# Row maxima of attention scores as b + relu(a - b) on two engines, and the output bias as a row added by TensorE

## Chip, cores and metric

One core of a Trainium2 chip runs the whole decoder layer. The time is the device time of one execution in microseconds. Three executions of the kernel before took 5262.17, 5269.80 and 5275.28 us, median 5269.8 us. The engines are called PE (TensorE), ACT (ScalarE), DVE (VectorE), POOL (GpSimd) and SP (SyncE, which here only issues DMAs). Each of them works its own queue in order.

## What is computed

Three sub-layers follow one another for x of shape (8, 512, 512). Each adds its result to its input and normalizes. The first is a selective state-space layer: a recurrence over 512 positions for 1024 channels with 16 states each. The second is cross-attention with 16 heads of 32. The third is a mixture of 32 experts with a shared expert. All is float32. The change is in the attention:

```python
qm = _split_heads(q @ Wq.T + bq)
km = _split_heads(k @ Wk.T + bk)
vm = _split_heads(v @ Wv.T + bv)
scores = jnp.einsum('bnlh,bnph->bnlp', qm, km) / np.sqrt(HEAD_DIM).astype(np.float32)
scores = jnp.where(mask, scores, MASK_FILL)
attn = jax.nn.softmax(scores, axis=-1)
out = jnp.einsum('bnlp,bnph->bnlh', attn, vm)
out = out.transpose(0, 2, 1, 3).reshape(B, L, D_MODEL)
return out @ Wo.T + bo
...
h = dA_t * h + dBx_t            # the recurrence of the first sub-layer, 512 positions
...
x = _layernorm(x + _L0_attn_ref(x, ...))
x = _layernorm(x + _L0_xattn_ref(x, ctx_1024, ctx_1024, mask_BxS2_bf1, ...))
x = _layernorm(x + _L0_ffn_ref(x, ...))
```

## The kernel before

Three functions run in turn. `layers` does the state-space layer, the attention, the shared expert and the choice of experts, `experts` the 32 experts, and `finish` the last normalization. The change touches `layers` alone.

`layers` goes over 16 chunks of 256 positions (8 batch rows, two chunks each). A chunk has 32 scan steps, 512 in all. One scan step (L1113 to L1208) is, in program order:

- `steps_in` (L494, DVE): the input of the recurrence, 128 x 1024, into a tile `h` (tag h, 6 buffers).
- `scan` (L501, DVE): the recurrence over 128 x 1028. It reads decays `l_da`, which has two buffers.
- `decays` (L480, ACT): four exponentials of 128 x 256 that fill the other decay buffer for the next step. They can start only when the scan that last read this buffer has ended.
- `collect` (L510, DVE): 128 x 1024, times C. Then `products` (L521, PE) folds pairs of `h` tiles into PSUM `py`, after which an `h` tile is free again.

Everything else is side work, put into the steps in small pieces. The attention and the shared expert of batch row b run beside the scans of row b + 1; for the last row they run after the last scan. `units(b)` lists those pieces with a weight each, and the step loop (L1148 to L1153) takes from the list in proportion to weights. The pieces of a step are dealt into thirds (L1154), and each third is issued by `run(m)`: the first before the scan, the second after the decays, the third after `collect`. `clock[0]` counts these thirds. A piece may return a function that is its second half; `settle` (L294) issues it when the next piece runs, or, where a pair (due, function) is returned, when `clock[0]` has reached `due`. The code is issued through a scheduler that settles the order on each engine when the kernel is built; at run time every engine takes its queue in that order and waits on semaphores.

The attention of one batch row has 8 head pairs, and each pair 4 blocks of 128 query rows. For pair i:

- `spread` (L799): DMAs put the pair's queries and keys into `qa` and `ka` (three sets of each). A head takes 64 rows: 32 of the head, one with the mask's fill `filld` in `ka`, one of ones in `ka` against the negated maxima in `qa`.
- `maximum` (L811): two matmuls (L819) make 128 x 2 x 512 scores `ps_s` in PSUM (tag sc, 2 buffers), and one DVE reduction (L821) takes the largest of each row and head into `mx`.
- `negate` (L823): transposes `mx` and puts it, negated, as a row into `qa`.
- `weigh` (L839): two matmuls (L845) make the scores again, transposed and with the maximum already subtracted, `ps_t` (same tag sc), and ACT takes their exponential into `eT` (L849; tag eT, 2 buffers).
- `gather` (L853): two matmuls (L861) multiply by the values.

A maximum, a weigh and a gather of different pairs stand together in the list (L997 to L1008), the maximum six blocks ahead. I call the three a group; there are 32 in a batch row and 256 in all, 224 of them beside scans.

`sources(b)` makes keys and values a row ahead and spills them to DRAM (`keys`, L732, four blocks per batch row). `output` (L908) multiplies by Wo through `dense` (L753) and adds the residual (L919) and the bias `bo` (L920), the latter a tile of 128 x 512 that holds the bias in every row. `biases` (L1037) prepares `bo` and `filld` once. `silu` (L391) is preceded and followed by a load of ACT's function table.

Of the kernel before, what the change touches and what calls it, by code (L numbers as in the profile page):

```python
# [8 lines left out]
F32 = mybir.dt.float32  # L9
# [8 lines left out]
P = 128  # L18
# [14 lines left out]
NB = 4  # L33
NPB = 3

NH = 16
# [53 lines left out]
def layers(ctx, tc, a, x1d, filld, based, xbuf, arm):  # L90
# [88 lines left out]
    w_x = const("w_x", [P, CC, RANK + 2 * NST], rows(a["x_proj_w"]))  # L179
    w_dt = const("w_dt", [RANK, DI], a["dt_proj_w"])  # L180
    b_dt = const("b_dt", [P, CC], a["dt_proj_b"])
# [4 lines left out]
    bv = cp.tile([P, DC], F32, name="l_bv")  # L186
    bo = cp.tile([P, D], F32, name="l_bo")
    wg = cp.tile([P, DC, E], F32, name="l_wg")
# [47 lines left out]
    for i in range(NPB):  # L236
        qas.append(cp.tile([P, S], F32, name=f"l_qa{i}"))
        kas.append(cp.tile([P, S], F32, name=f"l_ka{i}"))
        for t in (qas[i], kas[i]):
            for r0 in (HD, 2 * HD + HD):  # L240
                nc.gpsimd.memset(t[r0 : r0 + HD], 1.0 if t is qas[i] else 0.0)
# [21 lines left out]
    def later_constants():  # L263

        nc.sync.dma_start(
            aneg.rearrange("p c j g -> p (c j) g"),
            a["A_log"].rearrange("(b c) (s g) -> (c s) b g", c=QP, s=NQ),
        )
        for i in range(NPB):
            for r0 in (HD + 1, 2 * HD + HD + 1):  # L270
                nc.sync.dma_start(
                    kas[i][r0 : r0 + 1, :].rearrange("p (c t) -> p c t", c=DC),
                    ones[0:1, :].unsqueeze(1).to_broadcast([1, DC, P]),
                )
        nc.sync.dma_start(bq, a["bq"])
        nc.sync.dma_start(bk, a["bk"])
        nc.sync.dma_start(bv, a["bv"].rearrange("(c p) -> p c", p=P))
        nc.sync.dma_start(bo, a["bo"].partition_broadcast(P))
        nc.sync.dma_start(wg, rows(a["wg"]))
# [152 lines left out]
    def prepare(q, f):  # L432

        ps = psm.tile([P, 2, T], F32, tag="mm", name="ps_dt")
        for i in range(2):
            c = 2 * q + i
            nc.tensor.matmul(
                ps[:, i, :], w_dt[:, c * P : (c + 1) * P], f["xd"][0:RANK, :], start=True, stop=True
            )
# [267 lines left out]
    def sources(b):  # L707
# [3 lines left out]
        def begin():  # L711
            load("Wv")
            st["cT"] = cT = quad("s2", "cT")
            nc.sync.dma_start(cT, rows(a["ctx"][b]))
            st["mk"] = mk = p1.tile([P, S], U8, tag="mk", name="mk")
            nc.sync.dma_start(mk, a["mask"][b : b + 1, :].to_broadcast([P, S]))
            kept[b] = [dp.tile([S, D], F32, tag="vd", name="vd"), dp.tile([D, S], F32, tag="kd", name="kd")]

# [13 lines left out]
        def keys(oc):  # L732
            if oc == 0 and b:
                load("Wq")
            w, cT = loaded["Wk"], st["cT"]
            ps = dense(lambda dc: w[:, dc, oc * P : (oc + 1) * P], lambda dc: cT[:, dc, :])

            def put():

                k = p3.tile([P, D], F32, tag="row", name="k")  # L740
                nc.vector.scalar_tensor_tensor(k, ps, bk[:, oc : oc + 1], st["mk"], ALU.add, ALU.mult)
                nc.sync.dma_start(kept[b][1][oc * P : (oc + 1) * P, :], k)

            return put
# [7 lines left out]

    def dense(lhs, rhs):  # L753
        ps = psm.tile([P, S], F32, tag="mm", name="ps_p")
        for dc in range(DC):
            nc.tensor.matmul(ps, lhs(dc), rhs(dc), start=(dc == 0), stop=(dc == DC - 1))  # L756
        return ps

    def units(b):
# [39 lines left out]
        def spread(i):  # L799
# [3 lines left out]
            for j in range(2):  # L803
# [4 lines left out]
                nc.sync.dma_start(ka[r1 + HD : r1 + HD + 1, :], filld[b : b + 1, :])  # L808
                nc.sync.dma_start(qa[r1 + HD + 1 : r1 + HD + 2, :], ka[r1 + HD + 2 : r1 + HD + 3, :])

        def maximum(i, lt):  # L811
# [5 lines left out]
            for j in range(2):  # L817
                r = slice(j * 2 * HD, (j + 1) * 2 * HD)
                nc.tensor.matmul(ps[:, j, :], qa[r, lt * P : (lt + 1) * P], ka[r, :], start=True, stop=True)  # L819
            mx = st["mx", i]  # L820
            return lambda: nc.vector.tensor_reduce(mx[:, lt, :].unsqueeze(2), ps, AX.X, ALU.max) and None  # L821

        def negate(i):  # L823

            mx = st.pop(("mx", i))
            pm = psm.tile([P, S], F32, tag="mm", name="ps_m")
            for lt in range(SC):
# [80 lines left out]
        def output(lt):  # L908
# [6 lines left out]
            w, attT = loaded["Wo"], st["attT"]  # L915
            pp = dense(lambda dc: attT[:, dc, lt * P : (lt + 1) * P], lambda dc: w[:, dc, :])

            def add_up():
                nc.vector.tensor_tensor(xr, pp, xr, ALU.add)  # L919
                nc.vector.tensor_tensor(st["x2"][lt], xr, bo, ALU.add)  # L920
                if lt == SC - 1:
# [115 lines left out]
    def biases():  # L1037
# [6 lines left out]
        nc.vector.tensor_scalar(fl[0:B, :], fl[0:B, :], -1.0, 1e8, ALU.add, ALU.mult)  # L1044
        nc.sync.dma_start(filld, fl[0:B, :])

# [3 lines left out]
        for dc in range(DC):  # L1050
# [3 lines left out]
            )  # L1054
        nc.vector.tensor_tensor(bo, bo, psb, ALU.add)

# [544 lines left out]
def program(tc, a, out):  # L1601
    nc = tc.nc
    with tc.tile_pool(name="dram", bufs=1, space=DRAM) as dram, tc.tile_pool(name="one", bufs=1) as one:
        x1d = dram.tile([N, D], F32, name="x1d")
        filld = dram.tile([B, S], F32, name="filld")

# [42 lines left out]
```

## Time and profile before

| what | us |
|---|---|
| median of three runs (5262.17 to 5275.28) | 5269.8 |
| the profiled execution | 5265.16 |
| its span, first to last instruction | 5263.4 |
| DVE busy over the span | 4170.1 (79%) |
| PE busy | 4483.6 (85%) |
| ACT busy | 2584.7 (49%) |
| POOL busy | 587.0 (11%) |
| first to last scan (start of each) | 60.6 to 3517.8 |
| attention of the last row and its shared expert, then experts and last normalization | from about 3520 |

A group line of the profile reads: line of the code, engine, operation, output <- inputs, shape, count, then busy time and mean duration in ns, then the idle time of the engine just before these instructions and what ended it. Busy time counts overlap once; so durations of neighbours can add up to more than the time they take together. A window line gives busy time and number of instructions of PE, PE's weight loads, DVE, ACT and POOL in a stretch, then the granted PE clock, DMA share and GB/s. A line of the table of waits reads: who waited, for whom, total us, times, longest. For the timeline: start, length, engine, line and operation, with neighbours of one kind merged into "xN" and the idle time before it in brackets.

### The profile page before, as it was taken

What the parts mean: (1) busy time and instruction counts of PE and PEld (TensorE: products, weight loads), DVE (VectorE), ACT (ScalarE), POOL (GpSimd) and SP (SyncE); (2) the same over time, 40 slices, a digit from 0 to 9 for tenths busy, and PEclk for the clock granted to TensorE, in tenths of its full rate; (3) what the DMA queues carried; (4) which work ended last, traced back from release to release, by engine and by line L of the source; (5) the groups of instructions that cost most, each with busy time, mean ns of one, the idle gap of its engine ahead of it and who ended that gap; (6) DMA issues with size and microseconds to landing.
All of it is one profiled execution on the core that took longest, in us unless ns stands there. A gap on an engine that the chain in (4) does not pass through costs nothing. (4 is left out here: it accounts for less than half of the span.)

```text
span 5263.4 us, 54340 instructions
## 1 busy us (share of the span) xinstructions
PE 4483.6 (85%) x17184; PEld 2454.6 (47%) x17184; DVE 4170.1 (79%) x5333; ACT 2584.7 (49%) x5765; POOL 587.0 (11%) x426
## 2 busy tenths in 40 slices
PE   6768879888888988888898888878899999999895
PEld 3324234333423423343342343333478888877775
DVE  7999898989989998998999899883356666655555
ACT  5566565655556556565656656543222333323233
POOL 1000002001100200200020020010112111111111
PEclk8879999999998999999898999989899999999998
DMA  8885345435634634543473454433244444444344
GB/s 236 265 231 156 74 118 175 116 97 135 180 83 104 200 95 107 161 142 97 95 217 74 120 176 116 107 106 106 96 116 134 133 126 134 134 124 126 116 125 157
DMA packets 486437, 711.62 MB, mean 135 GB/s; under 512 B 121576, under 2 KB 205064, under 8 KB 483952
## 3 DMA queue, kind: packets, MB, share of 16 engines
q1 hardware_dynamic: 449984, 626.90, 41.8%
q0 software_dynamic: 33280, 67.81, 5.8%
q10 hardware_dynamic: 2736, 11.54, 0.5%
q8 instruction: 220, 3.60, 0.3%
q14 instruction: 217, 1.78, 0.1%
HBM read 391.24 MB, written 164.79 MB: 106 GB/s over the span
## 5 line engine op out<-in xcount | busy, mean ns | idle before, releaser
L480 ACT ACTIVATE l_da<-rep,l_aneg 128x256 f32<-128x256 f32 x2048 | 893.4, 499 | 948.1 <-DVE h L501 884.5
L501 DVE TENSOR_TENSOR_SCAN h<-l_da,h 128x1028 f32<-128x1028 f32 x512 | 1165.1, 2290 | 20.9 <-ACT l_da L480 18.3
L494 DVE TENSOR_TENSOR h<-rep,bc 128x1024 f32<-128x1024 f32 x512 | 613.9, 1216 | 107.7 <-PE py L521 90.7
L510 DVE TENSOR_TENSOR h<-h,bc 128x1024 f32<-128x1024 f32 x512 | 618.6, 1215 | 2.0
L521 PE MATMUL py<-h,l_fold 128*32 128x512 f32 x2048 | 370.8, 647 | 110.1 <-DVE h L510 92.3
L819 PE MATMUL ps_s<-l_ka,l_qa 64*128 64x512 f32 x1024 | 329.2, 714 | 139.8 <-DVE mx L821 139.4
L1334 PE MATMUL ps_h<-xT,w 128*128 128x224 f32 (+3 forms) x1536 | 376.4, 395 | 36.8 <-issue 29.7
L1427 POOL DMA_INDIRECT based<-y,xe x160 | 272.8, 1705 | 1157.8 <-ACT y L1406 432.4
L821 DVE TENSOR_REDUCE mx<-ps_s 128x2 f32<-128x1024 f32 x256 | 310.0, 1216 | 66.5 <-PE ps_s L819 66.2
L861 PE MATMUL po<-eT,l_va 128*64 128x512 f32 x1024 | 303.6, 674 | 47.5 <-ACT eT L849 42.9
L1334 PEld LDWEIGHTS ps_h<-xT,w 128*128 128x128 f32 x1536 | 293.3, 192 | 100.3 <-issue 41.6
L845 PE MATMUL ps_t<-l_qa,l_ka 64*128 64x512 f32 x1024 | 306.0, 669 | 23.9 <-ACT eT L849 23.3
L849 ACT ACTIVATE eT<-ps_t 128x1024 f32<-128x1024 f32 x256 | 258.7, 1015 | 128.7 <-PE ps_t L845 128.5
L694 POOL DMA_INDIRECT xbuf<-x2t,dest x128 | 217.2, 1697 | 863.2 <-DVE dest L679 762.4
L343 PE MATMUL ps_z<-xnT,wm 128*128 128x256 f32 x1024 | 237.7, 388 | 28.7 <-DVE o L561 23.7
L756 PE MATMUL ps_p<-x2T,wa 128*128 128x512 f32 x512 | 242.0, 627 | 20.5 <-ACT hT L950 13.8
L552 PE MATMUL po<-wm,zs 128*128 128x512 f32 x512 | 246.7, 636 | 13.4 <-DVE z L963 11.7
L1334 PE MATMUL ps_h<-t,s 128*128 128x224 f32 (+3 forms) x1024 | 247.4, 392 | 5.8 <-DVE hT L1355 5.8
L343 PE MATMUL ps_x<-xnT,wm 128*128 128x256 f32 x1024 | 245.6, 392 | 4.9 <-ACT xnT L332 2.8
L1355 DVE TENSOR_TENSOR hT<-ps_h,p 128x224 f32<-128x224 f32 (+3 forms) x128 | 55.3, 432 | 242.7 <-PE ps_h L1334 242.7
L343 PEld LDWEIGHTS ps_z<-xnT,wm 128*128 128x128 f32 x1024 | 194.9, 193 | 90.5 <-DVE o L561 37.0
L343 PEld LDWEIGHTS ps_x<-xnT,wm 128*128 128x128 f32 x1024 | 195.5, 195 | 81.6 <-issue 44.8
(239 smaller groups left out, 6971.3 us busy)
## 6 DMA issues: line engine op xcount, KB each, us to landing
w<-in_w SPq DMA_DIRECT2D x93, 1024.0 KB
wm<-in_in_proj_w SPq DMA_DIRECT2D x128, 512.0 KB
rep<-dt SPq DMA_DIRECT2D x256, 256.0 KB
rep<-dtx SPq DMA_DIRECT2D x256, 256.0 KB
xbuf<-zero SPq DMA_DIRECT2D x32, 1362.5 KB
xe<-xbuf SPq DMA_DIRECT2D x32, 1362.5 KB
wm<-in_out_proj_w SPq DMA_DIRECT2D x64, 512.0 KB
wa<-in_sw SPq DMA_DIRECT2D x24, 1024.0 KB
```

The costliest lines, as they stand in the source:

```text
L343: nc.tensor.matmul(ps[:, i, :], w[:, dc, i * P : (i + 1) * P], f["xnT"][:, dc, :], start=(dc == 0), stop=(dc == DC - 1),)
L480: nc.scalar.activation(da[:, n, 1:], dt[:, j, i, :], AF.Exp, scale=aneg[:, 2 * q + i, 2 * jj + j, g : g + 1])
L494: nc.vector.tensor_tensor(h[:, :, 1:], dtx.rearrange("p j i t -> p (j i) t"), f["bc", g][0], ALU.mult)
L501: nc.vector.tensor_tensor_scan(flat, da.rearrange("p n t -> p (n t)"), flat, 0.0, ALU.mult, ALU.add)
L510: nc.vector.tensor_tensor(h[:, :, 0:T], h[:, :, 1:], f["bc", g][1], ALU.mult)
L521: nc.tensor.matmul(f["py"][j * QP : (j + 1) * QP, :, :], fold, hs[j // 2][:, 2 * (j % 2) : 2 * (j % 2) + 2, 0:T], start=False, stop=g == N ...
L819: nc.tensor.matmul(ps[:, j, :], qa[r, lt * P : (lt + 1) * P], ka[r, :], start=True, stop=True)
L821: return lambda: nc.vector.tensor_reduce(mx[:, lt, :].unsqueeze(2), ps, AX.X, ALU.max) and None
L845: nc.tensor.matmul(ps[:, j, :], ka[r, kc * P : (kc + 1) * P], qa[r, :], start=True, stop=True)
L861: nc.tensor.matmul(po[j * 2 * HD : (j + 1) * 2 * HD, :], va[:, kc, i, j * HD : (j + 2) * HD], eT[:, j, :], start=(kc == 0), stop=(kc == SC ...
L1334: nc.tensor.matmul(ps, w[:, n, r * P : (r + 1) * P], x[:, n, 0:cols], start=not more and n == 0, stop=n == 1, skip_group_check=more,)
L1427: put = nc.gpsimd.indirect_dma_start(out=based, out_offset=bass.IndirectOffsetOnAxis(ap=xe.bitcast(I32)[:, j, D + E :], axis=0), in_=ys[j] ...
```

## The change

The keys of a row, 512 columns, get a third half beside them: `ka` grows to 768 columns, where the last 256 hold the first half less the second half (a - b). For that `keys` subtracts once more and spills a second DMA, and `filld` gets the same third half. `maximum` now multiplies by columns 256 to 767, so that PSUM holds b and a - b instead of a and b. ACT takes relu(a - b) of both heads into a tile `up` of tag eT (128 x 2 x 256). DVE then adds b to it and takes the row maximum, once for each head, by `tensor_tensor_reduce`. In the built program each of these stands as two DVE instructions: the operation over 128 x 256, and a second one that writes `mx` (128 x 1). `ramp` hands the DVE part back with a due time one third of a step on; `negate` issues whatever is still owed.

The output bias becomes one row of a 32-row block that lies in the spare rows of the tile `w_dt`, the other 31 being zero. `dense` adds it by a fifth matmul against 32 rows of ones, and `output` is left with one DVE addition instead of two.

```diff
-    w_dt = const("w_dt", [RANK, DI], a["dt_proj_w"])
+    w_dt = cp.tile([2 * RANK, DI], F32, name="l_w_dt")
+    nc.sync.dma_start(w_dt[0:RANK, :], a["dt_proj_w"])
+    bo = w_dt[RANK : 2 * RANK, 0:D]
+    nc.gpsimd.memset(bo, 0.0)
-    bo = cp.tile([P, D], F32, name="l_bo")
...
-        kas.append(cp.tile([P, S], F32, name=f"l_ka{i}"))
+        kas.append(cp.tile([P, S + HS], F32, name=f"l_ka{i}"))
...
                 nc.vector.scalar_tensor_tensor(k, ps, bk[:, oc : oc + 1], st["mk"], ALU.add, ALU.mult)
-                nc.sync.dma_start(kept[b][1][oc * P : (oc + 1) * P, :], k)
+                nc.sync.dma_start(kept[b][1][oc * P : (oc + 1) * P, 0:S], k)
+                less = p3.tile([P, D], F32, tag="row", name="less")[:, 0:HS]
+                nc.vector.tensor_tensor(less, k[:, 0:HS], k[:, HS:], ALU.subtract)
+                nc.sync.dma_start(kept[b][1][oc * P : (oc + 1) * P, S:], less)
...
-    def dense(lhs, rhs):
+    def dense(lhs, rhs, row=None):
         ps = psm.tile([P, S], F32, tag="mm", name="ps_p")
         for dc in range(DC):
-            nc.tensor.matmul(ps, lhs(dc), rhs(dc), start=(dc == 0), stop=(dc == DC - 1))
+            nc.tensor.matmul(ps, lhs(dc), rhs(dc), start=(dc == 0), stop=(dc == DC - 1 and row is None))
+        if row is not None:
+            nc.tensor.matmul(ps, ones[RANK : 2 * RANK, :], row, start=False, stop=True)
         return ps
...
-                nc.tensor.matmul(ps[:, j, :], qa[r, lt * P : (lt + 1) * P], ka[r, :], start=True, stop=True)
+                nc.tensor.matmul(ps[:, j, :], qa[r, lt * P : (lt + 1) * P], ka[r, HS:], start=True, stop=True)
             mx = st["mx", i]
-            return lambda: nc.vector.tensor_reduce(mx[:, lt, :].unsqueeze(2), ps, AX.X, ALU.max) and None
+
+            def ramp():
+                up = p2.tile([P, 2, S], F32, tag="eT", name="up")[:, :, 0:HS]
+                nc.scalar.activation(up, ps[:, :, HS:], AF.Relu)
+
+                def largest():
+                    for j in range(2):
+                        nc.vector.tensor_tensor_reduce(
+                            up[:, j, :], ps[:, j, 0:HS], up[:, j, :], 1.0, -3e38, ALU.add, ALU.max, mx[:, lt, j : j + 1]
+                        )
+
+                owed = st.setdefault(("owed", i), [])
+                owed.append(largest)
+                return (clock[0] + 1 if clock else 0), lambda: owed and owed.pop(0)()
+
+            return ramp
 
         def negate(i):
 
             mx = st.pop(("mx", i))
+            owed = st.pop(("owed", i))
+            while owed:
+                owed.pop(0)()
...
-            pp = dense(lambda dc: attT[:, dc, lt * P : (lt + 1) * P], lambda dc: w[:, dc, :])
+            pp = dense(lambda dc: attT[:, dc, lt * P : (lt + 1) * P], lambda dc: w[:, dc, :], bo)
 
             def add_up():
-                nc.vector.tensor_tensor(xr, pp, xr, ALU.add)
-                nc.vector.tensor_tensor(st["x2"][lt], xr, bo, ALU.add)
+                nc.vector.tensor_tensor(st["x2"][lt], pp, xr, ALU.add)
...
-        nc.sync.dma_start(filld, fl[0:B, :])
+        nc.sync.dma_start(filld[:, 0:S], fl[0:B, :])
+        less = p3.tile([P, D], F32, tag="row", name="less")[0:B, 0:HS]
+        nc.vector.tensor_tensor(less, fl[0:B, 0:HS], fl[0:B, HS:], ALU.subtract)
+        nc.sync.dma_start(filld[:, S:], less)
...
-        nc.vector.tensor_tensor(bo, bo, psb, ALU.add)
+        row = p3.tile([P, D], F32, tag="row", name="bo")[0:1, :]
+        nc.sync.dma_start(row, a["bo"].unsqueeze(0))
+        nc.vector.tensor_tensor(row, row, psb[0:1, :], ALU.add)
+        nc.sync.dma_start(bo[0:1, :], row)
```

More of the change, by code (lines that the diff above doesn't have):

```diff
@@ L34 @@
 NPB = 3
+HS = S // 2
 NH = 16
@@ L271, in later_constants @@
                 nc.sync.dma_start(
-                    kas[i][r0 : r0 + 1, :].rearrange("p (c t) -> p c t", c=DC),
+                    kas[i][r0 : r0 + 1, 0:S].rearrange("p (c t) -> p c t", c=DC),
                     ones[0:1, :].unsqueeze(1).to_broadcast([1, DC, P]),
@@ L277, in later_constants @@
         nc.sync.dma_start(bv, a["bv"].rearrange("(c p) -> p c", p=P))
-        nc.sync.dma_start(bo, a["bo"].partition_broadcast(P))
         nc.sync.dma_start(wg, rows(a["wg"]))
@@ L437, in prepare @@
             nc.tensor.matmul(
-                ps[:, i, :], w_dt[:, c * P : (c + 1) * P], f["xd"][0:RANK, :], start=True, stop=True
+                ps[:, i, :], w_dt[0:RANK, c * P : (c + 1) * P], f["xd"][0:RANK, :], start=True, stop=True
             )
@@ L716, in begin @@
             nc.sync.dma_start(mk, a["mask"][b : b + 1, :].to_broadcast([P, S]))
-            kept[b] = [dp.tile([S, D], F32, tag="vd", name="vd"), dp.tile([D, S], F32, tag="kd", name="kd")]
+            kept[b] = [dp.tile([S, D], F32, tag="vd", name="vd"), dp.tile([D, S + HS], F32, tag="kd", name="kd")]
         def values(pc):
@@ L808, in spread @@
                 nc.sync.dma_start(ka[r1 + HD : r1 + HD + 1, :], filld[b : b + 1, :])
-                nc.sync.dma_start(qa[r1 + HD + 1 : r1 + HD + 2, :], ka[r1 + HD + 2 : r1 + HD + 3, :])
+                nc.sync.dma_start(qa[r1 + HD + 1 : r1 + HD + 2, :], ka[r1 + HD + 2 : r1 + HD + 3, 0:S])
         def maximum(i, lt):
@@ L1604, in program @@
         x1d = dram.tile([N, D], F32, name="x1d")
-        filld = dram.tile([B, S], F32, name="filld")
+        filld = dram.tile([B, S + HS], F32, name="filld")
         based = dram.tile([N, D], F32, name="based")
```

## The prediction

> **What bounds the kernel now.** I read the busy time by stretches first, then the costliest groups, then the waits of DVE and ACT between 500 and 3400 us, then the timeline.
>
> ```profile
> 900.00:1400.00 500.00, 423.50 (x1530) 184.96 (x1529) 449.45 (x489) 297.51 (x667) 44.13 (x31) 0.95 0.49 133
> ...
> 3600.00:3700.00 100.00, 98.72 (x412) 29.64 (x408) 44.71 (x41) 44.20 (x53) 0.00 (x0) 1.00 0.17 43
> ```
>
> Beside scans (900 to 1400) DVE is busy 449 of 500 us, PE 424, ACT 298: DVE bounds, PE is close. In the last row's attention, without scans (3600 to 3700), PE is busy 98.7 of 100: PE bounds.
>
> ```profile
> L480 ACT ACTIVATE l_da<-rep,l_aneg 128x256 f32<-128x256 f32 x2048 | 893.4, 499 | 948.1 <-DVE h L501 884.5
> L501 DVE TENSOR_TENSOR_SCAN h<-l_da,h 128x1028 f32<-128x1028 f32 x512 | 1165.1, 2290 | 20.9 <-ACT l_da L480 18.3
> L494 DVE TENSOR_TENSOR h<-rep,bc 128x1024 f32<-128x1024 f32 x512 | 613.9, 1216 | 107.7 <-PE py L521 90.7
> ...
> L821 DVE TENSOR_REDUCE mx<-ps_s 128x2 f32<-128x1024 f32 x256 | 310.0, 1216 | 66.5 <-PE ps_s L819 66.2
> ```
>
> The reductions are 310 us of DVE. ACT has 948 us of idle time before its decays alone, but it is idle because its queue's head waits for a scan; whatever stands behind those decays waits too.
>
> ```profile
> DVE h L494 <- PE py L521: 90.5, 37, 6.8
> DVE m L74 <- ACT r L70: 31.3, 25, 3.2
> DVE dtx L457 <- ACT dtx L453: 28.0, 20, 3.1
> DVE xs L377 <- ACT xs L369: 24.2, 14, 3.4
> DVE h L501 <- ACT l_da L480: 16.9, 6, 3.4
> DVE mx L821 <- PE ps_s L819: 13.3, 15, 1.4
> DVE zs L535 <- ACT zs L394: 13.0, 6, 2.2
> ```
>
> Where DVE waits for ACT today, it loses 113 us in all (31.3 + 28.0 + 24.2 + 16.9 + 13.0). The maxima wait for PE only, and little.
>
> ```profile
> 519.71 2.07 DVE L377 SCALAR_TENSOR_TENSOR xs<-xp,l_cw,xs 128x256 f32<-128x256 f32 x5
> 521.69 1.22 DVE L494 TENSOR_TENSOR h<-rep,bc 128x1024 f32<-128x1024 f32 x1
> 522.83 2.35 DVE L821 TENSOR_REDUCE mx<-ps_s 128x2 f32<-128x1024 f32 x2
> ```
>
> Neighbours overlap: the reduction lasts 1.22 us, but two take 2.35, so it occupies DVE 1.13 us. Five operations of 256 columns take 2.07, that is 0.40 each. Additions of 1024 and 512 columns occupy 1.13 and 0.60, so 1.04 ns a column, and a plain one of 256 would be 0.33.
>
> **The change, part by part.** Time counts where DVE bounds: 7 of 8 rows, so 224 of 256 maxima and 28 of 32 `output` blocks.
>
> *The maxima on DVE.* Out: 1.13 us each. In: two operations of 256 columns and two reads of the accumulator. No such operation is in the trace. Low: 0.33 + nothing, 0.67 a maximum; no two-source row runs faster than 1.04 ns a column, so it can't be less. High: the scan's rate (2290 ns for 1028 columns, 2.2 ns each), 0.63 an operation, and 0.17 a read as DVE's smallest rows last (L63 171 ns, L65 173), 1.60. I take 0.36 (between 0.33 and 0.40) and 0.10, 0.92 a maximum: it is an addition of one PSUM and one SBUF source, as L919, whose 512 columns last 682 ns like SBUF alone. 224 x (0.92 - 1.13) = **-47 us** (-103 to +105).
>
> Two scalar_tensor_tensor rows with both float32 sources in SBUF show the plain rate:
>
> ```profile
> L457 DVE SCALAR_TENSOR_TENSOR dtx<-dtx,u 128x512 f32<-128x512 f32 x64 | 43.8, 684 | 36.6 <-ACT dtx L453 36.6
> ...
> L458 DVE TENSOR_TENSOR l<-l,dtx 128x512 f32<-128x512 f32 x64 | 43.7, 682 | 1.0
> ```
>
> The Trainium skill's Vector Engine (DVE) Microarchitecture Reference, section 7 (Points that are easy to get wrong), says that this form halves its throughput with two non-bf16 SBUF sources; here 684 stands beside 682 for the plain addition, so the row doesn't show it, and by the rule a maximum would be near 1.4 us and the sum 60 us slower instead of 47 faster. Its VectorE: DVE Perf Modes, Rules for kernel authors, advises few operations rather than many; the change puts four in place of one, which the 0.92 holds already.
>
> *The bias.* One addition of 512 columns less: 28 x 0.60 = **-17 us**. PE gets 32 more matmuls of 512 columns; 18 of L756 take 7.89 us, 0.44 each, 28 x 0.44 = 12 us. I cost it at nothing: PE is idle 15% beside scans. Without that cover it is +12.
>
> *Keys.* 32 more DVE subtractions of 256 columns: **+11 us** (32 x 0.33). Their 32 DMAs, and the 256 that carry 768 columns for 512, go on SP's queue and on DMA engines that are half idle (share 0.49): nothing, as what waits for them was issued two pairs ahead. `less` takes a second `row` buffer, so a later key block may wait for a landing; at most about 1 us each, as L741 lost 1.0 to a DMA once, +28 at worst.
>
> *ACT.* 224 relus of 512 columns. L389 copies 512 columns from PSUM in 571 ns; less the overlap (four 499 ns decays take 1.69 to 1.71, so 0.09) it is 0.5: 112 us, in a queue that is idle 40% beside scans. As work it costs nothing. In the built order 16 table loads of 1.28 us are gone (128 to 112), 20 us that ACT gains.
>
> *The new waits.* DVE now waits for ACT at each maximum, and all its queue behind it: scans, `collect`, the inputs. And since `up` and `eT` share two buffers, in the built order the exponential of a group waits for DVE's part of the maximum before it, and the next relu stands behind that exponential. The stretch of the order that I copy out here repeats for nearly every row: scan; `collect`; DVE's pair; two inputs; DVE's next pair. ACT stands between the same scan and that next pair's relu with four decays, a relu, a table load, four silus, a table load, an exponential, and the relu: 4 x 0.40 + 0.5 + 1.28 + 4 x 0.54 + 1.28 + 0.92 + 0.5 = 8.2 us. DVE has 1.13 + 0.92 + 1.13 + 1.13 = 4.3 us to do. So it waits 3.9 us. Before, the reduction there didn't wait for ACT.
>
> I counted this for every DVE instruction that waits for ACT up to the last scan, in both built orders: ACT's queue from the DVE result that gates it, up to the awaited result, less what DVE has queued in between, plus 0.15 for handing over (when positive). Before: 74 us. After: 212, of which 96 at 49 of 224 maxima, and more than before at the convolution (27 to 39), at L457's chain (10 to 31) and the small normalization operations (13 to 19). The rise is 138. The same count through PE rises by 52, from 34 to 86. The count for before is under the trace's 113, so it doesn't exaggerate singly; but waits overlap, and part of the new ones falls on the 90.5 us that DVE now waits for `py`. I take three quarters of ACT's rise and none of PE's: **+104 us**. Bounds: 0 (all in idle time) to 138 x 113/74 + 52 = 263.
>
> *The last row.*
>
> ```profile
> 3643.04 1.13 PE L819 MATMUL ps_s<-l_ka,l_qa 64*128 64x512 f32 x4
> ...
> 3644.21 1.23 DVE L821 TENSOR_REDUCE mx<-ps_s 128x2 f32<-128x1024 f32 x1 [1.23 <-PE ps_s L819]
> ...
> 3645.96 0.30 PEld L819 LDWEIGHTS ps_s<-l_ka,l_qa 64*128 64x128 f32 x4 [0.81 <-DVE mx L821]
> ```
>
> A group takes 2.92 us (3643.04 to 3645.96), and PE fills it. The circle of a score buffer is 1.17 + 1.23 = 2.4 now; it becomes 1.17 + 0.5 + 0.92 and two handovers of 0.15, 2.9: the cover is used up but not passed. 32 x 0.1 + 4 x 0.44 = **+5** (0 to 15).
>
> **Sum:** -47 - 17 + 11 + 104 + 5 = +56. The profiled execution took 5265.2; with the change 5321. The median of the runs lies 4.6 above it: **5326 us**.
>
> **Rivals.**
> - *The waits fall into idle time.* For it: DVE already idles 10% beside scans, and DVE's part is issued a third of a step late. Against: 49 places where ACT has more queued than DVE. Then -53 for DVE and about 5 for the last row: 5222; with the cheap read (-103) 5166.
> - *Gain and waits cancel*, within 0.3% (16 us, about what a measurement of this kernel can tell from no change): waits of 32 to 64 us.
> - *The reduce form runs at the scan's rate.* Place: DVE, at each maximum. For it: nothing shows the operation; against: L919. From 1.13 us a maximum on, the edit saves nothing; at 1.60 it costs +105 instead of -47: 5478.
> - *PE becomes the bound*: score buffers are held longer, PE's queue stops, `py` comes late and L494 waits. For it: PE is 85% busy and its count rises by 52. Then 5326 + 52 + 34 (the rest of ACT's rise) = 5412.
> - *No saving on DVE*, if operation and read are 0.40 and 0.17 (1.14, +2 for -47): 5326 + 49 = 5375, inside the forecast's own range.
>
> **How the numbers follow.** Forecast (slower by waits, 5287 to 5440) 0.45; waits hidden 0.31; cancel 0.11; scan's rate 0.06; PE 0.07. Faster 0.31, same 0.11, slower 0.58. The range leaves out the scan's rate, the upper end of the waits and the lower third of the hidden case: 5195 to 5430.
>
> **What would show it.** L821's place: two rows of about 0.45 us and two small ones; DVE's busy time beside scans down by some 50 us. DVE waiting for ACT at the maxima, near 100 us in all, and ACT's exponentials waiting for DVE, which they never did. The scan stage (first to last scan now 60 to 3518) longer while DVE's share of it falls. Wrong if DVE's waits for ACT stay near 113 us (then faster), or if a maximum occupies DVE for 1.13 us or more (then slower for another reason).

## The result and the profile after

The changed kernel takes 5277.8 us (median of 13 runs, 5273.0 to 5286.1); the kernel before took 5263.8 beside it (13 runs). The ratio is 1.0027, 95% interval 1.0020 to 1.0035: some 14 us slower, where the forecast said about 56. The profiled execution spans 5271.8 us, 8.4 more than the one before (5263.4).

First the same two stretches of the view by stretches, for the kernel after. The columns are length, busy time of PE, PEld, DVE, ACT and POOL with instruction counts, granted clock, DMA share and GB/s.

```profile
900.00:1400.00 500.00, 436.42 (x1558) 188.80 (x1557) 436.26 (x590) 313.53 (x702) 40.96 (x30) 0.94 0.48 135
3600.00:3700.00 100.00, 97.64 (x376) 30.57 (x374) 30.68 (x132) 53.45 (x75) 0.14 (x1) 0.99 0.29 90
```

Beside scans DVE falls from 449 to 436 of 500 us while PE and ACT rise. DVE is now as busy as PE, and neither is full. The last row is still PE's (97.6 of 100).

The costliest groups of the kernel after, and from the groups of DVE the accumulator reads, which are too small for the page:

```profile
L482 ACT ACTIVATE l_da<-rep,l_aneg 128x256 f32<-128x256 f32 x2048 | 901.5, 500 | 836.0 <-DVE h L503 711.0
L503 DVE TENSOR_TENSOR_SCAN h<-l_da,h 128x1028 f32<-128x1028 f32 x512 | 1166.5, 2288 | 6.3 <-ACT l_da L482 2.4
L496 DVE TENSOR_TENSOR h<-rep,bc 128x1024 f32<-128x1024 f32 x512 | 613.5, 1214 | 145.8 <-PE py L523 130.5
...
L835 DVE CUSTOM_DVE_ANT_0 up<-ps_s,up 128x256 f32<-128x256 f32 x512 | 195.0, 417 | 186.8 <-ACT up L831 185.4
...
L874 ACT ACTIVATE eT<-ps_t 128x1024 f32<-128x1024 f32 x256 | 259.6, 1017 | 96.5 <-DVE mx L835 78.6
```

```profile
L835 DVE DVE_READ_ACCUMULATOR2_ANT mx<- 128x1 f32 x512 | 41.9, 82 | 0.0
```

The 310 us of reductions have become 195 of additions with a running maximum and 42 of reads. DVE waits 185 us for the relu in the whole span, and the exponentials of L874 wait 79 us for DVE's maxima.

What a maximum occupies is read from starts, not from durations. DVE's timeline of the kernel after (start, duration, instruction):

```profile
1009.79 0.41 DVE L835 CUSTOM_DVE_ANT_0 up<-ps_s,up 128x256 f32<-128x256 f32 x1
1010.13 0.08 DVE L835 DVE_READ_ACCUMULATOR2_ANT mx<- 128x1 f32 x1
1010.13 0.41 DVE L835 CUSTOM_DVE_ANT_0 up<-ps_s,up 128x256 f32<-128x256 f32 x1
1010.48 0.08 DVE L835 DVE_READ_ACCUMULATOR2_ANT mx<- 128x1 f32 x1
1010.48 2.29 DVE L503 TENSOR_TENSOR_SCAN h<-l_da,h 128x1028 f32<-128x1028 f32 x1
```

The read and the next operation start at the same moment. So a maximum occupies 0.69 us (1009.79 to 1010.48), not 0.92.

Waits of DVE in the scan stage of the kernel after (61.7 to 3534.3; total, times, longest), and that stage's row by stretches:

```profile
DVE h L496 <- PE py L523: 130.5, 61, 6.5
DVE up L835 <- ACT up L831: 117.7, 49, 5.7
DVE m L75 <- ACT r L71: 41.2, 26, 4.5
DVE dtx L459 <- ACT dtx L455: 22.5, 15, 3.1
DVE zs L537 <- ACT zs L396: 13.3, 7, 2.2
...
DVE xs L379 <- ACT xs L371: 3.6, 4, 2.1
DVE h L503 <- ACT l_da L482: 2.4, 1, 2.4
```

```profile
61.70:3534.30 3472.60, 2905.76 (x10195) 1220.42 (x10194) 3087.51 (x4052) 2136.06 (x4803) 256.92 (x191) 0.92 0.51 140
```

The same stage before (60.6 to 3520.1), with two of its waits:

```profile
60.60:3520.10 3459.50, 2864.43 (x10166) 1220.63 (x10164) 3185.66 (x3382) 2040.93 (x4598) 271.24 (x191) 0.92 0.50 138
```

```profile
DVE h L494 <- PE py L521: 90.7, 38, 6.8
DVE m L74 <- ACT r L70: 31.5, 26, 3.2
```

It lasted 3459.5 us with DVE busy for 3185.7. So DVE lost 98 us of work and gained 111 us of idle time (273.8 to 385.1), and the stage grew by 13. The new wait for the relu has 118 us at 49 places; the one for `py` grew from 91 to 131, the one in the normalizations (`m`) from 32 to 41. The part from the start of the last scan on went from 1745.6 to 1739.8 us. A single profile is worth about 8 us here: another execution of the very same program (the run with two thirds of a step, below) had a scan stage of 3480.2 us for 3472.6.

### The profile page after: what moved, and what is told of

Read it like the earlier page. It is cut to its first block, busy times and chain, and to the rows that moved or that the text cites. A ratio compares the mean times of both kernels' runs of the same rounds, so it can differ in the third digit from the quotient of the medians.

```text
span 5271.8 us, 55880 instructions
## 1 busy us (share of the span) xinstructions
PE 4538.0 (86%) x17248; PEld 2454.8 (47%) x17248; DVE 4057.3 (77%) x6102; ACT 2701.0 (51%) x6005; POOL 574.1 (11%) x427
## 5 line engine op out<-in xcount | busy, mean ns | idle before, releaser
L496 DVE TENSOR_TENSOR h<-rep,bc 128x1024 f32<-128x1024 f32 x512 | 613.5, 1214 | 145.8 <-PE py L523 130.5
L523 PE MATMUL py<-h,l_fold 128*32 128x512 f32 x2048 | 392.9, 672 | 106.5 <-DVE h L512 90.3
L826 PE MATMUL ps_s<-l_ka,l_qa 64*128 64x512 f32 x1024 | 316.4, 684 | 158.1 <-DVE mx L835 153.6
L835 DVE CUSTOM_DVE_ANT_0 up<-ps_s,up 128x256 f32<-128x256 f32 x512 | 195.0, 417 | 186.8 <-ACT up L831 185.4
L874 ACT ACTIVATE eT<-ps_t 128x1024 f32<-128x1024 f32 x256 | 259.6, 1017 | 96.5 <-DVE mx L835 78.6
L826 PEld LDWEIGHTS ps_s<-l_ka,l_qa 64*128 64x128 f32 x1024 | 87.0, 192 | 322.4 <-issue 144.7
```

The lines of the kernel that those rows point to most:

```text
L496: nc.vector.tensor_tensor(h[:, :, 1:], dtx.rearrange("p j i t -> p (j i) t"), f["bc", g][0], ALU.mult)
L523: nc.tensor.matmul(f["py"][j * QP : (j + 1) * QP, :, :], fold, hs[j // 2][:, 2 * (j % 2) : 2 * (j % 2) + 2, 0:T], start=False, stop=g == N ...
L874: nc.scalar.activation(eT, ps, AF.Exp)
```

## Experiments

Differences in us are the difference of two ratios times 5264, the median before, so that runs taken at different times can be set side by side. The first guess was that the 14 us are a loss by waits, less gains of the bias and of the cheap maximum.

**The bias row alone** (the kernel before with only the change's bias part):

```diff
-            pp = dense(lambda dc: attT[:, dc, lt * P : (lt + 1) * P], lambda dc: w[:, dc, :])
+            pp = dense(lambda dc: attT[:, dc, lt * P : (lt + 1) * P], lambda dc: w[:, dc, :], bo)
...
-                nc.vector.tensor_tensor(xr, pp, xr, ALU.add)
-                nc.vector.tensor_tensor(st["x2"][lt], xr, bo, ALU.add)
+                nc.vector.tensor_tensor(st["x2"][lt], pp, xr, ALU.add)
```

> The kernel before with the bias row alone; maxima and keys as before. Theory A (DVE bounds beside scans, and what leaves its queue without a new wait is gained): 28 additions that occupy DVE 0.60 us each leave, so 17 us faster, 5240 to 5255 against about 5264. Rival B (PE's fifth matmul delays what stands behind it as much as DVE gains): within 8 us of the kernel before.

Measured: 5281.2 us, 1.0031 [1.0019, 1.0043]: 16 us slower instead of 17 faster. Its scan stage, and DVE's first waits in it:

```profile
61.10:3532.80 3471.70, 2910.04 (x10197) 1230.40 (x10196) 3171.03 (x3348) 2040.68 (x4594) 261.04 (x191) 0.91 0.50 138
```

```profile
DVE h L495 <- PE py L522: 100.8, 44, 7.0
DVE m L74 <- ACT r L70: 40.3, 26, 4.0
```

DVE has its 15 us less work (3185.7 to 3171.0), but the stage is 12 longer; PE is busy for 46 more. A loss of that size was there without a single relu.

**Buffers of its own for the relu:**

```diff
-                up = p2.tile([P, 2, S], F32, tag="eT", name="up")[:, :, 0:HS]
+                up = p2.tile([P, D], F32, tag="xr", name="up").rearrange("p (j k) -> p j k", j=2)
```

> The changed kernel with relu's result in two buffers of its own (the two of tag xr, idle during the maxima) instead of the two that it shares with the exponentials. In the built order 175 of 256 exponentials wait for DVE's part of a maximum in the changed kernel, and none here. Theory A1 (the 118 us that DVE waits for relu come mostly of this sharing, relu standing behind an exponential that stands behind DVE): the wait of DVE for relu falls under 60 us and the time to 5200 to 5240. Rival A2 (relu is late because of ACT's own queue, decays that wait for scans, and table loads): the wait stays above 90 us and the time at 5265 to 5285.

Measured: 5280.4 us, 1.0033 [1.0023, 1.0042]. DVE still waits 116.0 us for the relu, at 52 places. The shared buffers are not the cause. In the changed kernel's trace, ACT stands before a relu for want of scores in under 2 of the 118 us that DVE waits; some 29 are the relus themselves, and in the rest ACT is at instructions ahead of them or waits there. So the relu is late because of what stands before it in ACT's own queue.

**No relu.** ACT's relu is left out; DVE adds ones to b, so the maximum is over half the keys and carries no relu.

```diff
-                up = p2.tile([P, 2, S], F32, tag="eT", name="up")[:, :, 0:HS]
-                nc.scalar.activation(up, ps[:, :, HS:], AF.Relu)
+                pass
...
-                            up[:, j, :], ps[:, j, 0:HS], up[:, j, :], 1.0, -3e38, ALU.add, ALU.max, mx[:, lt, j : j + 1]
+                            junk[:, j], ps[:, j, 0:HS].rearrange("p (n k) -> p n k", n=2), two, 1.0, -3e38, ALU.add, ALU.max, mx[:, lt, j : j + 1]
```

> The changed kernel without relu: DVE adds a constant tile to b instead, so the maximum goes over half of the keys and ACT does nothing for it. Theory A (DVE's 98 us of saved work are real, and waiting for ACT takes them back): 5150 to 5190. Rival C (what DVE saves is taken back by PE, whose score buffers and in-order queue set the pace): 5230 or more, with more idle time of DVE before L496 for PE.

Measured: 5219.8 us, 0.9911 [0.9895, 0.9927]: 61 us under the changed kernel. The wait for the relu (118 us) is gone, and only about half of it comes back as time. Where the rest went is in DVE's waits of this run:

```profile
DVE h L496 <- PE py L523: 133.3, 64, 5.8
DVE m L75 <- ACT r L71: 41.6, 26, 4.6
DVE dtx L459 <- ACT dtx L455: 35.4, 17, 3.1
DVE h L503 <- ACT l_da L482: 28.0, 7, 4.8
DVE junk L836 <- PE ps_s L826: 14.0, 15, 2.1
```

Decays, `dtx` and scores (2.4, 22.5 and nothing in the changed kernel) now take 28, 35 and 14 us. This run's built order also has 14 more loads of ACT's function tables than the changed kernel's (123 and 109 in the traces, 1.28 us each), so ACT is relieved of the relus less 18 us.

**The relu made, but unread** (DVE reads ones, as above; the maximum is again over half the keys):

```diff
+                    junk = p2.tile([P, D], F32, tag="xr", name="junk").rearrange("p (j n k) -> p j n k", j=2, n=2)
+                    two = ones.unsqueeze(1).to_broadcast([P, 2, P])
```

> As the one without relu, but ACT does the relu into the shared buffers, and nobody reads it; DVE waits for PE alone, a score buffer is free when both have read it. Theory A (it is DVE's wait for the result that costs): 5160 to 5205, close to the one without relu. Rival D (it is ACT's added work of 112 to 150 us, which pushes decays and exponentials back): 5240 or more.

Measured: 5277.5 us, 1.0025 [1.0016, 1.0035], and DVE still waited 114.1 us for the relu. Relu and maximum read one PSUM tile, and in the trace none of the 256 maxima starts before its relu has ended; so the wait was still there and the run doesn't separate work from waiting. It was made again so:

**ACT's work without a wait.** ACT takes a relu of the same size of constants instead of scores; nothing reads it, and DVE's maximum is as in the run without relu.

```diff
-                nc.scalar.activation(up, ps[:, :, HS:], AF.Relu)
+                nc.scalar.activation(up.rearrange("p (n k) -> p n k", n=4), ones.unsqueeze(1).to_broadcast([P, 4, P]), AF.Relu)
```

> As the run without relu (maximum over half of the keys, DVE waits for PE alone), but ACT does a relu of the same size on constants for each maximum, which nobody waits for. Theory A (DVE's wait for relu, 118 us in the trace, is what takes the gain back): 5215 to 5235, as without relu. Rival D (ACT's 112 to 150 us of work in its queue delay decays and exponentials): 5255 or more.

Measured: 5260.9 us, 0.9993 [0.9984, 1.0002]. So of the relu's 61 us, 43 are there when nobody waits for it, and 18 come with the wait. Each of these runs has a built order of its own, though, and orders of the same instructions differ by up to 20 us (below): the 43 are clear of that, the 18 are not. DVE's waits in this run:

```profile
DVE h L496 <- PE py L523: 134.2, 58, 7.4
DVE m L75 <- ACT r L71: 43.9, 32, 4.1
DVE junk L837 <- PE ps_s L826: 41.4, 24, 5.3
DVE dtx L459 <- ACT dtx L455: 40.3, 14, 3.1
DVE h L496 <- DMA rep<-dtx: 19.1, 12, 2.7
```

Against the run without relu, DVE waits 27 us more for scores and 5 for `dtx`, and 23 less for decays (5.0 for 28.0); in all it is idle for 29 us more (366.5 for 337.8). The rows for scores would fit this chain: a relu in ACT's queue makes the exponentials behind it late; these free a score buffer, and PE's next scores come late. It was not tried by itself.

**The bias taken apart.** The kernel before with no bias addition at all (the output lacks the bias); the changed kernel without the matmul that adds the row (it lacks it too); the kernel before with POOL adding the bias to the residual ahead of time.

```diff
-                nc.vector.tensor_tensor(xr, pp, xr, ALU.add)
-                nc.vector.tensor_tensor(st["x2"][lt], xr, bo, ALU.add)
+                nc.vector.tensor_tensor(st["x2"][lt], pp, xr, ALU.add)
```

```diff
-            pp = dense(lambda dc: attT[:, dc, lt * P : (lt + 1) * P], lambda dc: w[:, dc, :], bo)
+            pp = dense(lambda dc: attT[:, dc, lt * P : (lt + 1) * P], lambda dc: w[:, dc, :])
```

```diff
             xr = st.pop(("xr", lt))
+            nc.gpsimd.tensor_tensor(xr, xr, bo, ALU.add)
```

> The kernel before without adding the output bias anywhere (it is left out; DVE does one addition a block). Theory P (the bias row cost 1.05 us of PE a block in the run with the bias alone, 29 us beside scans, and this PE time sets the pace there): 15 to 25 us faster than before, 5240 to 5250. Rival Q (one addition less on DVE only moves the wait to PE, whatever PE does): within 8 us of 5265.

> The changed kernel without the bias matmul (the bias is left out). Theory P: its PE time of 29 us is gone from the path, 5240 to 5255, that is 25 to 35 us under the changed kernel. Rival Q: within 8 us of the changed kernel's 5278.

> The kernel before with the bias added to the residual by POOL, ahead of the product with Wo, so that DVE adds once and PE does nothing more. Theory P: 5240 to 5255, as with the bias left out. Rival (POOL's addition is late, or takes DVE's reads): 5262 or more.

Measured: 5274.2 us, 1.0023 [1.0014, 1.0032]; 5271.5 us, 1.0017 [1.0007, 1.0027]; 5289.8 us, 1.0056 [1.0042, 1.0070]. The first is the surprise: 32 operations less on DVE and nothing in their place, and it is 12 us slower. With the bias row alone and the changed kernel these make a table (us over the kernel before):

| maxima | DVE adds the bias | PE adds it | nobody |
|---|---|---|---|
| reductions | 0 | +16 | +12 |
| relu and addition | not run | +14 | +9 |

Read across, PE's matmul costs 4 to 5 us. Read down, the maxima with all their waits gain 2 to 3. Both are well under what an order alone moves (below). And the step out of "DVE adds the bias" costs 12, with no work to explain it. In the kernel before without the bias addition, DVE is busy for 15 us less in the scan stage (3170.2 for 3185.7) and idle for 18 more (291.9 for 273.8), ten of them for `py` and eight in the normalizations:

```profile
DVE h L494 <- PE py L521: 100.7, 46, 7.0
DVE m L74 <- ACT r L70: 39.7, 25, 3.8
```

The second wait goes with the edit and not with an order: it is 29 to 32 us in the four orders of the kernel before that were run, and 39 to 45 in each of the sixteen runs in which DVE doesn't add the bias. So about half of the 15 us is back there, as waiting for ACT. The wait for `py` moves with the order (80 to 113 us in the kernel before). Both are read from the waits and were not tried by themselves.

POOL's addition is the dearest, and beside the run that leaves the bias out it shows where its time goes: on every engine the two have the same instructions in the same order, but for POOL's 32. Those last 1.77 us each. The DVE instructions that run beside them are 15.6 us longer in all (a scan of 2.27 us takes 3.30), and the run takes 17 us more.

**The predicted price of a maximum.** The changed kernel with a DVE addition of 160 columns, about 0.23 us, after each maximum, which makes it 0.92.

```diff
+                    more = p2.tile([P, D], F32, tag="xr", name="more")[:, 0:160].rearrange("p (n k) -> p n k", n=2)
+                    some = ones[:, 0:80].unsqueeze(1).to_broadcast([P, 2, 80])
+                    nc.vector.tensor_tensor(more, some, some, ALU.add)
```

> The changed kernel with one more DVE addition of 160 columns behind each maximum, some 0.23 us, which brings DVE's part from the 0.69 us that the trace shows to the 0.92 that the prediction took; results are the same. Theory S (the prediction's sum was right and only the size of DVE's part off: DVE time beside scans counts in full): 52 us over the changed kernel, about 5330. Rival F (a part of DVE's time there is cover, and only a third counts, as the 103 us that DVE saved without relu brought 38): 10 to 25 us, 5288 to 5303.

Measured: 5303.2 us, 1.0074 [1.0060, 1.0088], 25 us over the changed kernel. Its waits and its scan stage:

```profile
DVE h L496 <- PE py L523: 108.6, 49, 6.5
DVE up L835 <- ACT up L831: 108.1, 44, 5.7
```

```profile
61.30:3561.50 3500.20, 2921.94 (x10197) 1231.16 (x10196) 3137.04 (x4276) 2136.45 (x4803) 267.26 (x191) 0.92 0.50 139
```

DVE is busy for 49.5 us more (3087.5 to 3137.0) and waits 22 less for `py` and 10 less for the relu; its idle time falls by 22 in all (385.1 to 363.2). About half of what is added to DVE arrives at the end.

**The late maxima back to reductions.** The late relus stand at the same blocks of each row. Five of 32 (10, 14, 20, 23 and 28) are reduced by DVE as before.

```diff
+            whole = SC * i + lt in (10, 14, 20, 23, 28)
...
+            if whole:
+                return lambda: nc.vector.tensor_reduce(mx[:, lt, :].unsqueeze(2), ps, AX.X, ALU.max) and None
```

> The changed kernel, but five of the 32 maxima of a batch row (number 10, 14, 20, 23 and 28), at which DVE waited 103 of its 118 us for relu, are taken by the old reduction from columns 0 to 511. DVE gets 0.44 x 35 = 15 us more. Theory W (these waits count in full): 5175 to 5205. Rival F (they count by a third to a half, as what DVE does not wait for relu it waits for PE): 5230 to 5262, still under the kernel before. Rival O (the waits turn up at other maxima in the new order): 5265 to 5285.

Measured: 5304.9 us, 1.0080 [1.0061, 1.0098]. DVE waits 17.6 us for the relu instead of 117.7, as meant, but now 54.4 at the five reductions for their scores and 35.4 for `dtx` instead of 22.5. The scan stage is as long as in the changed kernel (3473.5 for 3472.6 us); in this profile the part after it is 25 us longer, among others with one wait of 46.7 us for PE in the experts that the changed kernel's profile lacks. Why that part is longer was not followed up.

**The same instructions in another order.** A weight in the list of side work is changed a little. The instructions stay (with one exception, named below the table), and the built order moves. First the weight of `maximum` (0.91 for 0.9), then of `output` (3.5 or 3.3 for 3.4), in the kernels before, changed, and with the bias row alone.

```diff
-            add(3.4, output, lt, dry=(lt == 0))
+            add(3.5, output, lt, dry=(lt == 0))
```

> The kernel before with the weight of a maximum 0.91 instead of 0.90, so that the same instructions stand in a slightly other order (some 200 rows of 8265 on DVE). Theory N (what an order brings or costs is small against the edits): within 5 us of the kernel before. Rival L (the kernel before stands in a favourable order, and any other costs 10 to 20 us, as leaving out the bias addition did): 5272 to 5285.

> The kernel before with the weight of an output block 3.5 instead of 3.4: again the same instructions in a slightly other order. Theory N: within 5 us of the kernel before. Rival L: 5272 to 5285.

> The changed kernel in another built order: the weight with which `output` is spread over the row is 3.5 for 3.4, every instruction and every number computed is as in the changed kernel. Theory W (the change costs its +14 us by its own work and waits): 5273 to 5283, ratio 1.002 to 1.004, DVE waiting for the relu 110 to 125 us in the scan stage. Rival O (a difference of some 10 us comes from the order alone, as in the kernel before, where this same edit gave +11): over 6 us away from the changed kernel's 5278, either way.

> The changed kernel with `output`'s weight 3.3 for 3.4, a third order. W: 5273 to 5283. O: the three orders of the changed kernel spread over 10 us or more, and DVE's wait for the relu in the scan stage differs between them by over 20 us.

> The kernel before with `output`'s weight 3.3 for 3.4, its fourth order (the others gave 5264, 5264 and 5276). W: 5258 to 5270, below every order of the changed kernel. O: the four orders of before and the three of after overlap, and before's mean is 5265 to 5275.

> The kernel before with the bias as a row that TensorE adds, and `output`'s weight 3.5: another order of the run that gave 5281. W (the matmul's two instructions of some 0.5 us and the scan stage's waits cost it): 5276 to 5286. O (that run's +17 was its order): 5258 to 5272.

| order | before | bias row alone | changed |
|---|---|---|---|
| as written (3.4) | 5263.8 | 5281.2, 1.0031 [1.0019, 1.0043] | 5277.8, 1.0027 [1.0020, 1.0035] |
| `output` 3.5 | 5276.2, 1.0025 [1.0015, 1.0035] | 5306.4, 1.0078 [1.0064, 1.0092] | 5280.8, 1.0035 [1.0022, 1.0048] |
| `output` 3.3 | 5255.8, 0.9985 [0.9976, 0.9993] | not run | 5294.2, 1.0057 [1.0044, 1.0071] |
| `maximum` 0.91 | 5264.2, 1.0000 [0.9990, 1.0010] | not run | not run |

Four orders of the kernel before lie 20 us apart, three of the changed kernel 16. The slowest of these three, with 3.3, is the exception: it has 14 more loads of ACT's function tables (123 for 109), 18 us of ACT, so that it is not order alone. Row by row the change costs 14, 5 and 38 us. Its three orders are all above the four of before, in the mean by 19 us (5284.3 less 5265.0). With a scatter of 8.5 us among orders the standard error of that is 6.5 us (8.5 times the root of 1/4 + 1/3), so how much the change costs is known to some 17 us either way (2.57 standard errors at five degrees of freedom), although each single ratio is known to about 5. Without the slowest, the mean of the changed kernel is 14 us over that of the kernel before. The bias row costs 16 and 28 us, and the maxima on top of it gain 2 and 23. The kernel before with `output` at 3.3 is the one full version that beats both kernels, the kernel before by 0.15%.

In the kernel before and with the bias row, what moves from order to order is above all DVE's wait for `py`. The waits of the kernel before with 3.3 and of the bias row with 3.5 show the two ends:

```profile
DVE h L494 <- PE py L521: 80.1, 36, 5.5
DVE dtx L457 <- ACT dtx L453: 34.3, 20, 3.1
```

```profile
DVE h L495 <- PE py L522: 122.1, 45, 6.8
DVE m L74 <- ACT r L70: 39.9, 26, 3.9
```

In the changed kernel that is not so: its slowest order, with 3.3, has the shortest wait for `py` of its three.

```profile
DVE up L835 <- ACT up L831: 123.8, 58, 5.7
DVE h L496 <- PE py L523: 118.2, 67, 4.8
```

**The distance between relu and maximum:**

```diff
-                return (clock[0] + 1 if clock else 0), lambda: owed and owed.pop(0)()
+                return 0, lambda: owed and owed.pop(0)()
```

> The changed kernel with VectorE's part due at once (0 for clock[0] + 1), not a third of a step later. Theory L (the distance between relu and maximum in the order decides how long DVE waits): DVE waits for the relu over 160 us in the scan stage where it waits 118, time above 5300. Rival M (the relu is late because of what stands before it in ACT's queue, the distance of a third of a step is small against it): wait 100 to 140 us, 5270 to 5295, the spread that orders alone gave.

> The changed kernel with VectorE's part due two thirds of a step later (clock[0] + 2). L: the wait for the relu falls under 80 us, the time to 5240 to 5265. M: the wait stays at 100 to 140 us or falls, and the score buffers held longer give it back at py and at the exponentials: 5270 to 5295.

Measured: 5277.1 us, 1.0022 [1.0013, 1.0032], and 5277.5 us, 1.0028 [1.0017, 1.0039], with 121.5 and 119.2 us of waiting for the relu. Neither tells what it was made for. The second turned out to be the changed kernel to the instruction on every engine, and the first differs from it in few places: the next piece of side work settles the maximum anyway. What the two give is the reproducibility of one built order: 5277.8 and 5277.5. Whether a real distance would help wasn't tried.

## The prediction against the result

**What held.** The change is slower, the time lies in the range, and the marks named at its end are there, only that DVE is busy for 98 us less and not for some 50. DVE waits for ACT at the maxima for 117.7 us, at 49 of 224 places; the count in the built order had said 96 us at 49. DVE's idle time rises by 111 us where the step "The new waits" said 104. That total is in part luck: the waits for ACT rose by 84 (120.4 to 204.7) instead of 104 and those for PE by 22 (127.1 to 149.4) instead of nothing, and at the convolution (`xs`, 24.2 to 3.6) and L457's chain (`dtx`, 29.7 to 22.5) they fell where the count had them rise. Its 0.15 us for handing over is shown by no row of the prediction; from ACT's end to the start of the DVE instruction that waited for it, the trace of the kernel before has 0.03 in the median. The exponentials wait for DVE, which they never did. Its "The last row" said +5 (0 to 15); the cover held, and the part from the last scan on is 6 us shorter, which is within what a single profile is worth. PE's scores in the timeline of the kernel after show it:

```profile
3642.21 1.13 PE L826 MATMUL ps_s<-l_ka,l_qa 64*128 64x512 f32 x4
...
3645.13 1.13 PE L826 MATMUL ps_s<-l_ka,l_qa 64*128 64x512 f32 x4
...
3648.07 1.13 PE L826 MATMUL ps_s<-l_ka,l_qa 64*128 64x512 f32 x4
```

A group still takes 2.92 to 2.94 us, as the 2.92 before: PE fills it.

**The step that failed in size: "The maxima on DVE".** It took 0.36 us an operation and 0.10 a read, 0.92 a maximum and -47 us. Measured are 0.345 and nothing, 0.69, and 224 x (0.69 - 1.13) = -99. The low bound of 0.67 was nearly the truth; most of the error was the read. It explains the difference in DVE's work (98 us less, where -47 - 17 + 11 = -53 was forecast), and with it the profile's account nearly closes: 56, less 45 for that, plus 7 for the waits (111 for 104), less 11 for the last row, is 7; the profiled executions differ by 8.4. This is bookkeeping, as a stage is as long as DVE's work and idle time in it; it doesn't say which edit made the idle time.

**The step with the wrong sign: "The bias".** It said -17, with PE's part at nothing. Its PE part counted instructions for matmuls: one float32 matmul is two of them in the groups (64 for 32), and the timeline of PE after shows what a pair occupies:

```profile
770.77 1.12 PE L763 MATMUL ps_p<-l_w_dt,l_ones 32*128 32x512 f32 x2
771.82 1.13 PE L761 MATMUL ps_p<-wa,attT 128*128 128x512 f32 x2
```

From 770.77 to 771.82 are 1.05 us, not 0.44, so PE gets 28 x 1.05 = 29 us beside scans, not 12; PE's busy time in the scan stage rises by 29 from the changed kernel without that matmul (2876 to 2906). But the runs with it take only 4 to 5 us longer, so "PE is idle" covered most of it, as far as orders let that be seen. What failed is the -17: DVE's 17 us were taken away and nothing came (+12 with no bias at all, +16 and +28 with the row). Seven to ten of these 17 us turned into DVE's longer wait in the normalizations in each of the four runs that change the bias alone (39 to 40 us, for 29 to 32 before). The rest is not settled: the +12 lies within the spread of before's own orders (-8 to +13), and so does nearly the +16. The +28 compares runs of one weight and is over that spread; what in it is work, and what the reshuffled order, is open.

**The step that was right for part of a wrong reason: waits.** The forecast put ACT's work at nothing and its lateness at 104. The run with unawaited work says 43 for the work and 18 for waiting on it, the latter within what an order moves. And the whole edit of the maxima, waits and keys included, which the forecast had at -47 + 11 + 104 = +68 beside scans, is -2 in one order and -23 in the other: its gain and its waits cancel, as the rival of that name said, and the measured +14 (0.27%) is within its 0.3%. (Both are larger than that rival had them: 99 us and 118.) So the kernel is slower as forecast, but in neither comparison does the forecast's reason account for the net loss; it came with the bias edit and the order that this edit brings. For the third order, where the change costs 38, the bias row alone was not run.

**The sum itself.** It added DVE's work and DVE's waits as if each were time at the end. Two runs say that they are not independent: 49.5 us of work added give 25, as DVE's idle time shrinks by 22; and taking away 118 us of waiting gives 61. With -99 for -47 the sum would have been +4, near the measured +14, but with the bias 33 us wrong (+16 for -17) and the maxima 18 to 39 wrong the other way (+16 for -2 and -23).

**Rivals.** "The waits fall into idle time" fell: 118 us of them are there. "The reduce form runs at the scan's rate" fell (417 ns for 256 columns, under 0.63 us). So did "No saving on DVE" (0.69 for 1.14). "Gain and waits cancel" came true, by larger amounts than it had. "PE becomes the bound" fell as it was priced, but `py`, the largest wait already, grew from 90.7 to 130.5 us.

The Trainium skill's Vector Engine (DVE) Microarchitecture Reference, section 7, speaks of halved throughput of scalar_tensor_tensor with two non-bf16 sources in SBUF. The operation that came has one source in PSUM and stands in the trace as a custom one, so that the rule is not about it; its 0.345 us stand beside 0.33 for a plain addition of 256 columns, and nothing is halved here. The skill's VectorE: DVE Perf Modes, Two Vector instructions with no wait between them, says that an operation that writes its accumulator out is two instructions; the trace agrees (512 and 512). The second one takes no time of the engine here.

The skill's Perfetto Trace Analysis, Optimizing Scalar/DVE Operations, says that offloading to ScalarE may make sense where DVE is saturated. DVE was busy for 449 of 500 us and got 98 us back in the scan stage; the runs without and with ACT's work put what it cost here at 43 us for the work and 18 for the wait.

## To carry to other kernels

In a tightly coupled static order, work taken off the busiest engine is partly turned into waiting there (about half of the bias addition's 15 us went into the normalizations; of 49.5 us put back, 25 arrived), so price an edit with a discount and look for the next wait, here `py`. An engine that is idle 40% of the time is not free: unawaited work in its queue cost 43 us; other engines' results stand behind it. And where another order of the same instructions moves the time by up to 20 us, an edit worth less than that is to be tried in several orders before anything is said of its parts.

## What the hardware showed beside that

- The accumulator read of the reducing addition lasts 82 ns and occupies nothing: the next operation starts with it (1010.13 both).
- A bias matmul of 32 rows is not shorter on PE than its neighbours of 128 rows (1.05 us from 770.77 to 771.82; the pair before, of 128 rows, started at 769.71, 1.06 earlier; pairs of 128 rows in an unbroken run start 0.86 apart, 774.89 to 775.75).
- An addition of 128x512 on POOL, 1.77 us, makes DVE's instructions beside it longer: 15.6 us over 32 of them, against a run with the same order without them; one scan took 3.30 us for 2.27.
